# Layer-0 self attention of six tiles: softmax weights turned in 32x32 blocks by VectorE and moved between partitions by transfers, and a planner that chooses its pass by length and thinness

## The chip, the cores and the metric

The kernel runs on one core of a Trainium2 chip. The metric is the device time of one execution in microseconds. The kernel before was run ten times: median 2908.72 us, lowest 2903.48, highest 2914.35. Beside these there is one profiled execution of it.

## The reference

The program is a whole decoder of four layers on 32 sequences of 64 tokens with 256 features. Each layer adds self attention (or a state-space mixer in its place), cross attention to a context, and a feed-forward part to `x`, each on a layer-normalised `x`:

```python
x = x + _L0_attn_ref(_layernorm(x, axis=-1), L0_attn_wq, L0_attn_wk, L0_attn_wv, L0_attn_wo, ...)
x = x + _L0_xattn_ref(_layernorm(x, axis=-1), ctx_1024, mask_BxS2_bf1, ...)
x = x + _L0_ffn_ref(...)
...
```

The part that the change touches is the first line. With 32 query heads, 8 key and value heads and a head size of 64, what it returns is

```python
q, k = _apply_rope(q, cos, sin), _apply_rope(k, cos, sin)
scores = jnp.einsum('bhqd,bhkd->bhqk', q, k) / jnp.sqrt(jnp.float32(HD))
scores = jnp.where(causal[None, None], scores, jnp.finfo(scores.dtype).min)
probs = jax.nn.softmax(scores, axis=-1)
o = jnp.einsum('bhqk,bhkd->bhqd', probs, v)
return o.transpose(0, 2, 1, 3).reshape(b, s, NH * HD) @ wo.T
```

The weights `probs` come out with the queries on the partitions. The product with `v` sums over keys, and TensorE sums over partitions, so each block of weights has to be turned before that product.

## The kernel before

The 2048 tokens are 16 tiles of 128 rows, two sequences in each. `x` stays in the on-chip memory the whole time. A *unit* is one layer part on one or two tiles. `body` (from line 2606) records the units in an order of its own: the tiles go in groups of 8, 6 and 2 (`GROUPS`), and while a later group goes through the wide parts of layers 0 and 1, the group before it goes through the rest; `weave` mixes the two streams by shares. The first group has nothing beside it: its layer-0 self attention on tiles 0 to 7, then its layer-0 cross attention, stand alone at the start of the program.

Nothing is issued while units are recorded. The `Recorder` keeps each instruction with what it reads and writes, and the names of its buffers. Afterwards a planner, `Order`, simulates the five queues (TensorE, VectorE, ScalarE, GpSimd, and SP, which issues transfers) with a price for each instruction (`duration`), a start-up time for transfers, and a number of buffers per pool (`Net.SLOTS`): ten large ones of 4 KB a partition (`b4`), sixteen of 2 KB (`b2`), eight PSUM banks (`mm`), and others. It may look 120 us of TensorE's work ahead of the oldest unfinished instruction. An instruction with two possible engines (`either`: VectorE or ScalarE; `combine`: VectorE or GpSimd) is given to the one that ends first. Where TensorE would wait for more than 1.6 us and a bank is free, `fill` puts in a product that nobody reads (`spare`). A transfer is priced at 0.45 us on SP, and its result is held to be there 2 us or more later.

`in_turns` runs this planner forwards and backwards in alternation: each pass is renumbered by the one before it. With `rounds` 4 there are nine passes, of which five are forward. The forward pass with the shortest planned length is issued; all queues of the program then follow its order. On the chip, each queue works strictly in that order, waiting on semaphores.

All instructions are issued at one place (`issue`, line 2541), so the profile tells them apart by the names of tiles, which come from the function that made them.

A unit of layer-0 self attention (`unit_L0_attn`) works on tile `i`: a norm, projections with the rotation (`rope_mm`, `rope_b`), scores of 64x64 blocks into four PSUM banks, and then for each half `u` a softmax over a buffer of 128 partitions x 16 x 64. The partitions hold the queries. The scaled weights of a half are then turned by `turn`: eight 128x128 transposes on TensorE into two PSUM banks (`turn_mm`) and two evictions of 128x512 into one `b4` buffer (`turn_b`). The products with `v` read that buffer, 64 partitions at a time, two blocks of 128 columns for each:

```python
pT = self.turn(ss[u].rearrange("p a b -> p (a b)"), 8)
...
nc.tensor.matmul(po[64 * j : 64 * j + 64, hi, :], v[rb, kv * 64 : kv * 64 + 64],
                 pT[rb, j * 4 + hi * 2 : j * 4 + hi * 2 + 2, :], start=True, stop=True)
```

In cross attention the weights are turned differently, in 32x32 blocks by VectorE (`blocks`, tile name `blocks_b`), and the product takes the context's rows in strips of 32.

Of the kernel before, what the change touches and what calls it, by code (L numbers as in the profile page):

```python
# [26 lines left out]
P = 128  # L27
# [200 lines left out]
def split(ap, a, pat="p (a b) -> p a b"):  # L228
    return ap.rearrange(pat, a=a)
# [238 lines left out]
def part(method, args):  # L468

    if method == "transpose":  # L470
        return 128, 128
    return tuple(32 if n <= 32 else 64 if n <= 64 else 128 for n in (args[1].n, args[1].size()))
# [66 lines left out]
class Order:  # L539
# [81 lines left out]
    def run(self):  # L621
        ready = {e: [] for e in self.ENGINES}

        def enter(op):
            for e, _ in op.ways:
                bisect.insort(ready[e], op, key=lambda o: o.at)

        for o in self.ops:
            if o.waits == 0:
                enter(o)  # L630
        stuck, done, oldest, result, self.starts = False, [False] * len(self.ops), 0, [], {}
        while not all(done[oldest:]):
            limit = self.pos[oldest] + self.horizon
            best = None
            for e in self.ENGINES:
                now, seen, first = self.free_at[e], 0, 1e9
                for o in ready[e]:
# [9 lines left out]
                    start = max(now, since)  # L647
# [28 lines left out]
                    best = ((key, o.at), o, e, start, cost, opens)  # L676
# [7 lines left out]
            _, o, e, start, cost, opens = best  # L684
            filler = self.fill(o, start) if e == "tensor" else None
            if filler:
                o, start, opens = filler, self.free_at[e], []
# [9 lines left out]
            m = next(m for w, m in o.ways if w == e)  # L697
# [8 lines left out]
            if e == "scalar":  # L706
                m = next(m for w, m in o.ways if w == e)
# [14 lines left out]
            for n in o.after:  # L722
                same = len(n.ways) == 1 and n.ways[0][0] == e and o.ways[0][1] not in DMA
                at = (start if e in ("tensor", "sync") else got + 0.03) if same else got + lat
# [2 lines left out]
                n.waits -= 1  # L727
                if n.waits == 0:
                    enter(n)
            if not filler:  # L730
                done[o.at], self.starts[o] = True, (start, len(result))
            while oldest < len(done) and done[oldest]:
                oldest += 1
# [48 lines left out]
        o.after = before[o]  # L782


def in_turns(ops, slots, horizon, spare, rounds):

    best, ops = None, list(ops)
    for k in range(2 * rounds + 1):
        plan = Order(ops, slots, horizon, spare)
        result = plan.run()  # L790
        if k % 2 == 0 and (best is None or plan.length < best[0]):
            best = plan.length, result, {t: t.slot for o, _ in result for t in o.tiles}
        if k < 2 * rounds:
            backwards(ops)
            renumber(ops, plan.starts)
            rewind(ops)
    for t, slot in best[2].items():
        t.slot = slot
    return best[1]


class Net:
# [200 lines left out]
    def blocks(self, p, n):  # L1003
# [2 lines left out]
        self.nc.vector.transpose(pT.rearrange("p a h q -> p h a q"), p.rearrange("p h (a k) -> p h a k", a=2))  # L1006
        return pT

    def turn(self, p, n):

        pT = self.b4(n, P)
        for j in range(0, n, 4):
            ps = split(self.mm(), 4)
            for u in range(4):
                self.transpose(ps[:, u, :], p[:, (j + u) * P : (j + u + 1) * P])
            self.evac(pT[:, j : j + 4, :], ps)
        return pT
# [19 lines left out]
    def unit_L0_attn(self, layer, W, i):  # L1037
        nc = self.nc
        wq, wkv, wo = W
        cos, sin = (bc(v, 1, 8) for v in (self.k("rope0")[:, :64], self.k("rope0")[:, 64:]))  # L1040

        def rope(q, hT, cols):

            ps = self.mm()
            for x in range(4):
                self.prod(ps[:, x * P : (x + 1) * P], [(w, hT[:, c, :]) for c, w in enumerate(cols(x))])
            p3, t1, t2 = split(ps, 8), self.tmp(8, 64), self.tmp(8, 64)
            nc.vector.tensor_tensor(t1, p3, cos, ALU.mult)
            for j in range(4):
                at, of = (slice(32 * a, 32 * a + 32) for a in (j, j ^ 1))  # L1050
                self.evac(t2[at], p3[of])
            nc.combine(t2, t2, sin, ALU.mult)
            nc.combine(q, t1, t2, ALU.add)

        hT = self.norm(layer, [i])

        kk = self.b2(4, 2, 64)
        rope(kk.rearrange("p m b n -> p (m b) n"), hT, lambda x: [wkv[:, c, x * P : x * P + P] for c in range(2)])
        qs = [self.b4(2, 4, 2, 64) for _ in range(2)]
        for m in range(4):  # L1060
            rope(
                qs[m // 2][:, m % 2].rearrange("p g b n -> p (g b) n"), hT,
                lambda x: [wq[c][:, (4 * m + x) * P : (4 * m + x + 1) * P] for c in range(2)],
            )
        pv = self.mm()
        self.prod(pv, [(hT[:, c, :], wkv[:, c, 512:]) for c in range(2)])
        v = self.b2(512)
        self.evac(v, pv)

        sc = [self.mm() for _ in range(4)]  # L1070
        for u in range(2):
            for hi in range(2):
                for gp in range(2):
                    for b in range(2):
                        col = slice((hi * 2 + gp) * P + b * 64, (hi * 2 + gp) * P + b * 64 + 64)

                        for j in range(2):
                            r = slice(64 * j, 64 * j + 64)
                            for x in range(2):
                                nc.tensor.matmul(  # L1080
                                    sc[2 * u + j][64 * x : 64 * x + 64, col],
                                    qs[hi][r, u, 2 * gp + x, b],
                                    kk[r, 2 * hi + u, b],
                                    start=True,
                                    stop=True,
                                )
        ss = []
        for u in range(2):

            s = self.b4(16, 64)  # L1090
            for j in range(2):
                nc.vector.tensor_tensor(
                    s[:, 8 * j : 8 * j + 8], split(sc[2 * u + j], 8), bc(self.k("causal"), 1, 8), ALU.add
                )
            self.shift(s, s)
            nc.scalar.activation(s, s, AF.Exp, scale=0.125)
            r = self.weigh(s, s)
            nc.combine(s, s, bc(r, 2, 64), ALU.mult)
            ss.append(s)
        terms = []  # L1100
        for u in range(2):

            pT = self.turn(ss[u].rearrange("p a b -> p (a b)"), 8)

            oT = self.b4(2, 4, P)
            for b in range(2):
                po = split(self.mm(), 2)
                rb = slice(64 * b, 64 * b + 64)
                for hi in range(2):
                    for j in range(2):  # L1110
                        kv = hi * 4 + 2 * u + j
                        nc.tensor.matmul(
                            po[64 * j : 64 * j + 64, hi, :],
                            v[rb, kv * 64 : kv * 64 + 64],
                            pT[rb, j * 4 + hi * 2 : j * 4 + hi * 2 + 2, :],
                            start=True,
                            stop=True,
                        )
                self.evac(
                    oT[:, :, :, b * 64 : b * 64 + 64],  # L1120
                    po.rearrange("p h (g n) -> p h g n", n=64),
                )
            terms += [(oT[:, hi, c, :], wo[hi][:, u * 4 + c, :]) for hi in range(2) for c in range(4)]
        ps = self.mm()[:, :256]
        self.prod(ps, terms)
        self.outproj(i, ps)
# [1479 lines left out]
def body(tc, ins, out):  # L2606
    net = Net(ins, out)
    net.warm(8)
    for i in range(2):
        net.start(i)  # L2610

    at, before, ffn = 0, [], ["L1_queues"]
    for k, n in enumerate(GROUPS):
        tiles = range(at, at + n)
        wide = WIDE if k == len(GROUPS) - 1 else WIDE[:-1]
        if before:
            if wide is not WIDE:
                net.queues[at] = net.far(f"queue{k}", 8 * n * P, 256)
            early = NARROW[:4] if wide is WIDE else []
            weave(run_stages(net, ffn + NARROW, before), run_stages(net, wide + early, tiles))  # L2620
        else:
            weave(run_stages(net, wide[:2], tiles))
            net.queues[at] = net.far(f"queue{k}", 8 * n * P, 256)
            weave(run_stages(net, wide[2:4], tiles))
            net.slots = net.far("slots", 64 * P, ROW)
            weave(run_stages(net, wide[4:], tiles))
            net.parts = net.far("parts", 6 * QUEUED, 256)
        at, before = at + n, tiles

    net.all_experts, net.nc.quick = net.load_L3_experts(), True  # L2630
    weave(run_last(net, NARROW[4:-1], before), net.experts(QUEUED // P))
    issue(tc, in_turns(net.nc.ops, Net.SLOTS, 120.0, net.spare, 4), Net.SLOTS)


# [15 lines left out]
```

## Time and profile before

| what | value |
|---|---|
| median of ten runs | 2908.72 us (2903.48 to 2914.35) |
| profiled execution | 2915.26 us, span 2913.5 us |
| mean granted TensorE clock | 0.974 |
| busy: TensorE products | 2805.7 us |
| busy: VectorE | 2129.8 us |
| busy: ScalarE | 1518.5 us |
| busy: GpSimd | 1525.7 us |
| DMA | 259.04 MB, mean 89 GB/s |
| instructions | 66660 |

The page is one execution on the chip. A busy share is the time in which an engine had an instruction in work. Products are pipelined, so their listed durations overlap; what TensorE pays for one of a series is the spacing of their starts. The granted clock is the share of full speed at which TensorE was allowed to run, averaged over a slice. "Idle before" is the time that an engine stood still before an instruction, and the name behind the arrow is what released it. SPq is the queue that issues transfers. DMA times "to landing" go from the issue to the arrival of the data.

### The profile page before, as it was taken

To read this page: it belongs to the slowest core of one execution; us is meant where nothing else is said; L and a number is where in the kernel's file an instruction comes from. 1 tells how busy PE (TensorE), PEld (TensorE's weight loads), DVE (VectorE), ACT (ScalarE), POOL (GpSimd) and SP (SyncE) were. 2 spreads that over 40 slices of the span, in tenths; PEclk is the share of its full clock that TensorE was granted. 3 is DMA by queue.
4 is the path that set the end of the run, shared out by engine and by line. 5 is a ranking of instruction groups with operands and counts; after the bars stand their busy time and mean duration, and the time that the engine had idled before them with its cause. 6 is when DMAs were issued, how large, how long until landed. Compare 5 with 4: busy or idle time off the path is not lost.

```text
span 2913.5 us, 66660 instructions
## 1 busy us (share of the span) xinstructions
PE 2805.7 (96%) x26626; PEld 2338.6 (80%) x26626; DVE 2129.8 (73%) x5139; ACT 1518.5 (52%) x2849; POOL 1525.7 (52%) x1304
## 2 busy tenths in 40 slices
PE   8999999999999899999999999999999999999895
PEld 7888888878778788888878778878797878877674
DVE  5664457775777767867589998787846879988853
ACT  5554226665445454544366656665534665376550
POOL 6762232212666545424554437685715477457665
PEclk8999999999999999999999999999999999998977
DMA  4003320400261146122100110022374122211435
GB/s 179 16 13 116 139 109 19 156 1 31 81 259 46 57 152 203 62 64 69 46 17 30 33 56 17 8 96 77 127 263 171 57 73 82 89 51 58 143 113 176
DMA packets 120313, 259.04 MB, mean 89 GB/s; under 512 B 27077, under 2 KB 81880, under 8 KB 107588
## 3 DMA queue, kind: packets, MB, share of 16 engines
q1 hardware_dynamic: 110212, 230.68, 22.8%
q0 software_dynamic: 9792, 24.10, 2.4%
q8 instruction: 211, 3.46, 0.5%
q14 instruction: 98, 0.80, 0.1%
HBM read 179.38 MB, written 78.77 MB: 89 GB/s over the span
## 4 chain that ended last, share of the span: by engine, by line
PE 78%; DVE 11%; ACT 6%; POOL 2%; issue 2%; DMA 0%; SPq 0%; POOLq 0%; DVEq 0%; ACTq 0%
PE L_xattn_mm L2541 13%; PE ssm_heads_mm L2541 11%; PE pair_mm L2541 10%; PE cross_out_mm L2541 9%; PE L_attn_mm L2541 7%; PE L_ffn_mm L2541 5%; PE L_block_mm L2541 3%; PE rope_mm L2541 2%; PE turn_mm L2541 2%; DVE rope_b L2541 2%; PE L_dense_mm L2541 2%; PE cross_scores_mm L2541 2%; PE heads_mm L2541 2%; ACT rope_b L2541 2%; PE small_scores_mm L2541 1%
## 5 line engine op out<-in xcount | busy, mean ns | idle before, releaser
L2541 PE MATMUL pair_mm<-norm_b,load_ssm_w 128*128 128x256 f32 x1280 | 307.1, 381 | 1.5 <-DVE __init___x L2541 0.5
L2541 PEld LDWEIGHTS pair_mm<-norm_b,load_ssm_w 128*128 128x128 f32 x1280 | 235.0, 190 | 36.8 <-issue 4.5
L2541 POOL TENSOR_TENSOR L_xattn_sm<-L_xattn_sm,__init___consts 128x8 f32<-128x8 f32 (+2 forms) x64 | 190.5, 2983 | 57.2 <-DVE L_xattn_sm L2541 50.4
L2541 DVE SCALAR_TENSOR_TENSOR ssm_heads_b<-pair_mm,load_ssm_wp,ssm_heads_b 128x252 f32<-128x252 f32 (+2 forms) x480 | 196.9, 465 | 22.5 <-ACT ssm_heads_b L2541 21.4
L2541 ACT COPY rope_b<-rope_mm 32x512 f32<-32x512 f32 x234 | 134.7, 577 | 115.7 <-DVE rope_b L2541 71.9
L2541 POOL TENSOR_TENSOR norm_sm<-norm_sm,__init___consts 128x1 f32<-128x1 f32 (+1 forms) x149 | 93.9, 640 | 169.3 <-DVE norm_sm L2541 149.8
L2541 ACT ACT_TABLE_LOAD x136 | 174.5, 1283 | 10.7 <-DVE L_xattn_sm L2541 2.6
L2541 ACT COPY L_xattn_b<-L_xattn_mm 128x512 f32<-128x512 f32 x177 | 103.8, 591 | 130.9 <-PE L_xattn_mm L2541 128.0
L2541 PE MATMUL rope_mm<-norm_b,load_L_attn_w 128*128 128x128 f32 x1280 | 163.1, 282 | 4.3 <-DVE rope_b L2541 2.7
L2541 PEld LDWEIGHTS rope_mm<-norm_b,load_L_attn_w 128*128 128x128 f32 x1280 | 155.6, 197 | 13.8 <-issue 8.1
L2541 PE MATMUL ssm_heads_mm<-load_ssm_w,ssm_heads_b 128*128 128x256 f32 x640 | 160.0, 384 | 0.2 <-DVE ssm_heads_b L2541 0.2
L2541 ACT ACTIVATE ssm_heads_b<-ssm_heads_b 128x512 f32<-128x512 f32 (+1 forms) x152 | 124.3, 833 | 51.3 <-DVE ssm_heads_b L2541 37.0
L2541 POOL TENSOR_TENSOR ssm_heads_b<-ssm_heads_b,ssm_heads_b 128x1024 f32<-128x1024 f32 x33 | 80.7, 2451 | 134.4 <-DVE ssm_heads_b L2541 115.8
L2541 PEld LDWEIGHTS ssm_heads_mm<-load_ssm_w,ssm_heads_b 128*128 128x128 f32 x640 | 116.5, 190 | 23.1 <-issue 9.3
L2541 POOL TENSOR_TENSOR rope_b<-rope_b,__init___consts 128x512 f32<-128x512 f32 x72 | 93.2, 1296 | 79.2 <-DVE rope_b L2541 37.3
L2541 ACT COPY turn_b<-turn_mm 128x512 f32<-128x512 f32 x194 | 106.4, 602 | 53.2 <-PE turn_mm L2541 50.4
L2541 DVE TENSOR_SCALAR norm_b<-__init___x,norm_sm,norm_sm 128x256 f32<-128x256 f32 x192 | 104.8, 565 | 31.5 <-POOL norm_sm L2541 9.6
L2541 PEld LDWEIGHTS L_xattn_mm<-norm_b,load_L_xattn_w 128*128 128x128 f32 x1024 | 121.1, 192 | 7.8 <-issue 5.9
L2541 ACT COPY norm_b<-norm_mm 128x256 f32<-128x256 f32 (+1 forms) x133 | 56.9, 436 | 133.1 <-PE norm_mm L2541 118.7
L2541 POOL TENSOR_TENSOR heads_b<-heads_b,heads_sm 128x1024 f32<-128x1024 f32 x52 | 102.0, 1969 | 45.6 <-DVE heads_sm L2541 26.0
L2541 PE MATMUL L_xattn_mm<-norm_b,load_L_xattn_w 128*128 128x128 f32 x1024 | 125.4, 276 | 0.0
L2541 PEld LDWEIGHTS L_xattn_mm<-norm_b,units_L_xattn_w 128*128 128x128 f32 x1024 | 119.9, 192 | 3.3 <-issue 1.0
(439 smaller groups left out, 7895.4 us busy)
## 6 DMA issues: line engine op xcount, KB each, us to landing
L_block_w<-in_f_rows SPq DMA_DIRECT2D x42, 770.0 KB, 5.9
queue<-far_w SPq DMA_DIRECT2D x14, 1024.0 KB, 10.7
load_ssm_w<-in_s_in SPq DMA_DIRECT2D x12, 1024.0 KB, 6.4
parts<-far_w SPq DMA_DIRECT2D x10, 1024.0 KB, 17.1
slots<-far_w SPq DMA_DIRECT2D x16, 548.0 KB, 7.7
L_experts_b<-slots SPq DMA_DIRECT2D x32, 274.0 KB, 5.1
units_L_xattn_w<-kept_x SPq DMA_DIRECT2D x8, 1024.0 KB, 7.9
L_parts_b<-parts SPq DMA_DIRECT2D x14, 512.0 KB, 8.5
```

The source lines that it names most:

```text
L2541: done = getattr(getattr(nc, e), method)(*map(real, op.args), **kw)
```

## The change

It has three parts.

First, for tiles 2 to 7 (six tiles of the first group) `turn` is replaced by `moved`. VectorE turns the whole buffer of a half, 128 partitions x 1024, in blocks of 32x32 within strips of 32 partitions, into a `b4` buffer `y`. Sixteen transfers, issued by SP, then carry block row `a` of column block `b` to partitions 32b to 32b+31 of a second `b4` buffer `z`; each is 32 partitions x 1 KB. The other ten tiles keep `turn`.

Second, the product's view of the turned weights is rewritten so that it fits both: runs of 32 queries, four of them to a block of 128. The numbers in PSUM lie as before.

Third, the planner's choice. `in_turns` gets 8 rounds instead of 4: 17 passes, nine of them forward. Instead of the shortest, the pass with the least `plan.length + THIN * thin(plan)` is issued. `thin` cuts the plan into stretches of 3.413 us, adds up TensorE's planned work in each, fillers included, and counts the stretches with less than 36% of work. `THIN` is 3 us a stretch.

```diff
         stuck, done, oldest, result, self.starts = False, [False] * len(self.ops), 0, [], {}
+        self.fills = []
...
-            if not filler:
+            if filler:
+                self.fills.append(start)
+            else:
                 done[o.at], self.starts[o] = True, (start, len(result))
...
+STRETCH, FULL, THIN = 3.413, 0.36, 3.0
+
+def thin(plan):
+    work = {}
+    for o, (start, _) in plan.starts.items():
+        if o.ways[0][0] == "tensor":
+            k, m = part(o.ways[0][1], o.args)
+            n = o.args[2].size() * 0.00167 * k * m / P**2 if o.ways[0][1] == "matmul" else 0.107
+            at = int(start / STRETCH)
+            work[at] = work.get(at, 0.0) + n
+    for start in plan.fills:
+        work[int(start / STRETCH)] = work.get(int(start / STRETCH), 0.0) + 0.43
+    return sum(work.get(i, 0.0) < FULL * STRETCH for i in range(max(work)))
...
-        if k % 2 == 0 and (best is None or plan.length < best[0]):
-            best = plan.length, result, {t: t.slot for o, _ in result for t in o.tiles}
+        worth = plan.length + THIN * thin(plan)
+        if k % 2 == 0 and (best is None or worth < best[0]):
+            best = worth, result, {t: t.slot for o, _ in result for t in o.tiles}
...
+    def moved(self, p, n):
+        y, z = self.b4(4, n, 32), self.b4(4, n, 32)
+        self.nc.vector.transpose(y.rearrange("p b j q -> p j b q"), p.rearrange("p (j b k) -> p j b k", j=n, b=4))
+        for b in range(4):
+            for a in range(4):
+                self.nc.sync.dma_start(out=z[32 * b : 32 * b + 32, a], in_=y[32 * a : 32 * a + 32, b])
+        return z.rearrange("p a j q -> p j a q")
...
-            pT = self.turn(ss[u].rearrange("p a b -> p (a b)"), 8)
+            p = ss[u].rearrange("p a b -> p (a b)")
+            pT = self.moved(p, 8) if i in range(2, 8) else self.turn(p, 8).rearrange("p j (a q) -> p j a q", q=32)
...
-                            po[64 * j : 64 * j + 64, hi, :],
+                            po[64 * j : 64 * j + 64, hi, :].rearrange("p (g a q) -> p g a q", g=2, q=32),
...
-    issue(tc, in_turns(net.nc.ops, Net.SLOTS, 120.0, net.spare, 4), Net.SLOTS)
+    issue(tc, in_turns(net.nc.ops, Net.SLOTS, 120.0, net.spare, 8), Net.SLOTS)
```

## The prediction

> **What bounds the kernel now.** I read the page's busy shares first, then the granted clock in slices, then a table of stages, and inside the first stage the tiles of the turned weights and the order in time. The page:
>
> ```profile
> PE 2805.7 (96%) x26626; PEld 2338.6 (80%) x26626; DVE 2129.8 (73%) x5139; ACT 1518.5 (52%) x2849; POOL 1525.7 (52%) x1304
> ...
> PEclk8999999999999999999999999999999999998977
> ...
> PE 78%; DVE 11%; ACT 6%; POOL 2%; issue 2%; DMA 0%; SPq 0%; POOLq 0%; DVEq 0%; ACTq 0%
> ```
>
> TensorE is busy for 2805.7 of 2913.5 us and carries 78% of the chain of waits. All its idle time is 107.8 us; nothing but less TensorE work, less of that idle time, or less time at a reduced clock can move the end much. The stages (stretch, length, then busy us and count for PE, PEld, DVE, ACT, POOL, then granted clock, DMA share, GB/s):
>
> ```profile
> 0.00:250.00 250.00, 235.99 (x2512) 208.40 (x2513) 148.37 (x250) 134.70 (x238) 162.00 (x124) 0.95 0.22 78
> 250.00:900.00 650.00, 649.04 (x5487) 534.97 (x5486) 417.62 (x938) 299.47 (x522) 228.59 (x163) 1.00 0.26 97
> 900.00:1250.00 350.00, 328.73 (x3176) 284.01 (x3178) 275.44 (x650) 180.87 (x337) 189.82 (x158) 0.98 0.34 111
> 1250.00:1950.00 700.00, 689.64 (x6861) 572.50 (x6854) 565.94 (x1360) 408.65 (x778) 379.77 (x336) 1.00 0.12 41
> 1950.00:2150.00 200.00, 192.17 (x1754) 160.62 (x1753) 151.23 (x412) 100.97 (x198) 119.03 (x97) 0.95 0.37 127
> 2550.00:2913.50 363.50, 312.52 (x3238) 246.73 (x3236) 251.00 (x739) 179.63 (x364) 231.80 (x228) 0.88 0.33 108
> ```
>
> Layer-0 self attention of the first eight tiles lies in the first row. TensorE idles 14.0 us there, 21.3 from 900 to 1250, and 51.0 in the last row, which also has the worst clock. A finer cut shows how the clock is lost:
>
> ```profile
> 60.00:70.00 10.00, 9.37 (x126) 8.99 (x127) 9.70 (x18) 5.33 (x9) 7.96 (x7) 0.66 0.01 2
> 170.00:180.00 10.00, 8.76 (x78) 7.17 (x79) 7.00 (x9) 4.53 (x7) 7.69 (x6) 0.66 0.09 28
> 1500.00:1510.00 10.00, 7.71 (x83) 6.87 (x84) 7.37 (x17) 4.36 (x7) 5.73 (x4) 0.66 0.01 2
> 2650.00:2660.00 10.00, 8.09 (x84) 6.09 (x83) 8.70 (x18) 7.61 (x21) 10.00 (x8) 0.50 0.01 2
> ```
>
> A clock of 0.66 over 10 us is 3.4 us of full-speed time lost. Adding (1 - clock) x 10 us over all 10 us slices gives 12 us before 250, 20 us in seven separate places from 900 to 2550, and 31 us from 2640 to 2880. That, 51 us behind the first stage, is what a choice by thin stretches can reach for.
>
> **The turned weights, removed.** Six tiles lose 16 turns each, 96 in all:
>
> ```profile
> L2541 PE MATMUL turn_mm<-__init___consts,L_attn_b x256: 272/273/447, 72.1 to 2115.1; 128*128 128x128 f32 x128
> L2541 ACT COPY turn_b<-turn_mm x194: 562/591/767, 75.7 to 2800.1; 128x512 f32<-128x512 f32 x194
> ...
> 82.68 0.87 PE turn_mm L2541 x8
> ...
> 114.69 1.04 PE L_attn_mm L2541 x16
> ```
>
> 256 turns are 16 tiles' worth. The 273 ns are a pipelined matmul's length; the chain shows what TensorE pays, 0.87 us for eight, 0.109 each. So 96 x 0.109 = 10.5 us of TensorE's work go. With them go 24 evictions x 0.591 = 14.2 us, mostly ScalarE's, which is busy 112 of the 200 us from 50 to 250, and that is worth nothing by itself.
>
> **What VectorE gets.** Two block turns per tile, priced by the same shape in cross attention:
>
> ```profile
> L2541 DVE STREAM_TRANSPOSE blocks_b<-L_xattn_b x32: 1196/1235/1247, 269.4 to 2461.3; 128x1024 f32<-128x1024 f32 x32
> ```
>
> 12 x 1.235 = 14.8 us. From 50 to 250 VectorE is busy 121 of 200 us, so it has room: cost 0. If its order were tight, as from 60 to 70 where it is busy 9.7 of 10, a turn there would cost its 1.2 us; twelve times that, 15 us, is the upper end.
>
> **What the transfers cost.** Each half of a tile issues 16 transfers of 32 partitions x 1 KB, 192 in all, 6.3 MB. The trace has no transfer between partitions of the on-chip memory. Nearest rows: issues one behind another on SP, and small transfers' landing:
>
> ```profile
> 329.34 0.43 SPq L2541 DMA_DIRECT2D load_ssm_ws<-in_s_in  x1
> 329.81 0.47 SPq L2541 DMA_DIRECT2D load_ssm_wp<-in_s_dtb  x1
> ...
> context_cx<-in_ctx SPq DMA_DIRECT2D x64, 64.0 KB, 2.0
> ```
>
> One issue per 0.47 us makes 16 x 0.47 = 7.5 us per half, 15 us per tile, 90 us of SP. The turned weights are whole 1.24 + 7.5 + 2.0 = 10.7 us after the scaled weights, against 0.87 + two evictions of 0.59, about 2 us, before: 8.7 us later. The 2.0 us can be 1.7 (output rows) or, behind bulk loads, 17.1 (zeros into the queue of parts); DMA is at 0.00 to 0.01 between 50 and 120, so I take 2.0. Does the delay show? In the order in time, taking the turns in pairs as tiles, tile 4's turns are at 154 and 156 and their products at 166 to 174, tile 7's at 236 and 240 and theirs after 250: there some 10 us lay between anyway. Tile 2's turns at 96 and 105 had products at 101 and 115, and tile 3's at 128 and 131 had them at 132 and 136, so there it must be covered by the next tile's projections, about 7 us (60 at 0.11), and its scores. A tile passes every 21 us (72 to 240 for eight). I take 0, because the planner sees the transfer's length and may run ahead; the upper end is 8.7 us for each of six tiles, 52 us.
>
> A rule speaks against this. The Trainium skill, "VectorE: DVE Perf Modes", section "Rules for kernel authors", tells authors to turn 128x128 on TensorE where a PSUM destination will do, and keeps VectorE for 32x32 blocks. Followed, it would count the 10.5 us as no gain and the later weights as a loss, up to 52 us. Another, "DMA: Bandwidth & Descriptors", section "Rules for kernel authors", says that a transfer under 64 KB is mostly overhead, with some 2.0 us fixed by its section on the anatomy of a DMA; taken in series, 192 would be an estimated 384 us. The rows put 0.47 us between issues, so the fixed parts overlap.
>
> SP is in order: behind a transfer that waits for VectorE's turn stand the operand loads of layer-0 cross attention (128 to 191 us) and its contexts from 210. SP idles most of 50 to 128 and 138 to 191, so I charge 0. POOL's queue issues nothing more.
>
> **Buffers.** The pool of ten large buffers gives two to a half instead of one, the added one from VectorE's turn to the last transfer's end, some 10 us. A tile holds two for queries, two for scores, two for outputs; next tile's two queries still fit. I charge 0; if they do not, the stall is in the 52 us above.
>
> **The products of the turned weights** read runs of 32 instead of 128. No row shows that shape; 16 such products take 1.04 us now, and the element count is unchanged, so 0; were they to take double, 6 x 32 x 0.065 = 12.5 us more. Nothing suggests a gain.
>
> **What of the 10.5 us reaches the end.** In 60 to 80 and 160 to 180, 40 of the 190 us, TensorE was not the limit; there it buys nothing. 10.5 x 150/190 = 8.3, I take 8 us. From 250 to 900 TensorE idles 1 us, so time won before is passed on, not lost in a later wait.
>
> **The pass.** Nine forward passes instead of five are compared, by length plus 3 us per thin stretch, and the chosen one orders the whole program anew. The most to be had is 51 us of clock and the idle time with it. A thin stretch removed is worth 3.4 us of clock at most, and up to 3 us of planned length may be paid for it. I take four fewer at about 2 us net, 8 us. Ends: 0 (the shortest is also the least thin) or a loss of 12 (four paid for with 3 us, none seen on the chip), and 35 us if most of the 51 go.
>
> **Sum.** The profiled execution took 2915.3 us, 1.8 more than its span. 2915.3 - 8 - 8 = 2899.3. It was 6.5 us above the median 2908.7, so a median of 2892.8: 2893.
>
> **Rivals.**
> - *A luckier order.* The half-clock stretches in 2640 to 2880 and at 950, 1505 and 2003 go, 25 us instead of 8, beside the 8 of TensorE: 2876. For it: the last stage has 31 us of lost clock in some eight places. Against it: that stage ends narrow, with 51 us of idle that no reordering removes while work is missing.
> - *Hidden both ways.* The 10.5 us turn into idle time, since the weights are late by as much, and the pass gives nothing: 2908.7 within 5.8 us, which is the 0.2% that a measurement of this kernel can tell from no change. For it: two stretches of the stage are already bound by the elementwise chain. Against it: the other 150 us.
> - *Late weights stall TensorE (slower).* From 50 to 240, with TensorE waiting for transfers or for a large buffer. Decides from 1.74 us of stall per moved tile (what 16 turns save), plus 3.4 us whenever the gap also drops the clock. At 3 us of stall and one clock drop in each of six tiles: 6 x 6.4 - 8 = 30, less 8 for the pass, +22: 2931. For it: tile 2's products came 5 to 10 us after their turn, tile 3's 4 and 5. Against it: the gaps of tiles 4 and 7.
> - *The choice does nothing.* The pass of least worth is also the shortest: 2915.3 - 8 - 6.5 = 2901, still slightly faster.
>
> **How the numbers follow.** Forecast 0.32 (2886 to 2898); choice does nothing 0.10, all but its upper edge faster; luckier order 0.18; hidden 0.14; slower 0.26. Faster is 0.32 + 0.10 + 0.18 = 0.60, same 0.14, slower 0.26, for which an order that is worse elsewhere counts too. To leave out two in ten I go from 2866 (luckier order with 35 instead of 25) to 2932 (the stall's price). The likeliest case's own range is 2886 to 2898.
>
> **What would show it.** Right: 96 fewer turns and 192 more issues on SP in the changed trace, 12 block turns at 1.2 us, TensorE's busy time 10 us less, fewer 10 us slices under 1.0. Wrong: idle TensorE before the products of the turned weights released by a transfer; clock below 0.95 in the first 250 us; issues well above 0.5 us; products above 0.066 us each; more idle time after 900 than the 93 us of now.

## The result, and the profile after

The changed kernel takes 2943.72 us (median of 13 runs, 2931.8 to 2956.11) against 2910.64 us for the kernel before (45 runs): ratio 1.0114, 95% interval 1.0100 to 1.0129. It is 33 us slower. The forecast was 2893 us, faster.

The page after, its own lines of the span, of busy time, of TensorE's clock in 40 slices, and of one group of products:

```profile
span 2945.8 us, 66818 instructions
...
PE 2826.7 (96%) x26536; PEld 2354.6 (80%) x26536; DVE 2131.7 (72%) x5122; ACT 1526.4 (52%) x2867; POOL 1513.4 (51%) x1294
...
PEclk9999999999999899999999999999899999998997
...
L2572 PE MATMUL pair_mm<-norm_b,load_ssm_w 128*128 128x256 f32 x1280 | 315.4, 390 | 0.0
```

The last group in the page before:

```profile
L2541 PE MATMUL pair_mm<-norm_b,load_ssm_w 128*128 128x256 f32 x1280 | 307.1, 381 | 1.5 <-DVE __init___x L2541 0.5
```

TensorE has 90 instructions fewer (96 turns gone, 6 filler records more) and is busy 21 us longer. Its work did not grow: products that the change does not touch, such as `pair_mm`, take longer in the mean (390 ns, 381 before), because more of them run at half clock. The mean clock fell from 0.974 to 0.964. As time lost that is (1 - 0.974) x 2913.5 = 76 us before and (1 - 0.964) x 2945.8 = 106 us after, 30 us more. TensorE's idle time went from 107.8 to 2945.8 - 2826.7 = 119.1 us, 11 us more. With 10.5 us of work less, 30 + 11 - 10.5 = 31 us, against 32.3 us between the two spans. So the whole loss is clock and idle time.

Where is it? Fixed stretches of time hold different work in the two kernels, so I cut both where TensorE has the same work still to come (its products without fillers, each at the spacing of its shape in the kernel before). The rows have length, busy time of PE, PEld, DVE, ACT and POOL, granted clock, DMA. The kernel before:

```profile
0.00:386.90 386.90, 372.89 (x3842) 328.44 (x3846) 215.29 (x380) 174.14 (x319) 198.54 (x148) 0.97 0.27 97
386.90:1012.90 626.00, 615.94 (x5222) 504.21 (x5215) 443.87 (x1045) 320.51 (x559) 262.44 (x194) 0.99 0.22 83
1012.90:1665.90 653.00, 634.78 (x5861) 539.45 (x5861) 503.18 (x1197) 342.88 (x643) 316.62 (x288) 0.99 0.23 75
1665.90:2334.60 668.70, 655.31 (x6253) 543.26 (x6248) 527.09 (x1347) 385.09 (x725) 377.62 (x331) 0.98 0.27 95
2334.60:2913.50 578.90, 526.77 (x5461) 423.24 (x5459) 440.33 (x1173) 295.92 (x606) 370.47 (x345) 0.92 0.30 98
```

The changed kernel:

```profile
0.00:387.40 387.40, 368.93 (x3755) 321.59 (x3756) 227.47 (x375) 176.46 (x320) 194.66 (x144) 0.96 0.33 116
387.40:1040.20 652.80, 638.52 (x5272) 520.99 (x5271) 439.89 (x1050) 323.01 (x557) 265.34 (x198) 0.97 0.21 78
1040.20:1681.90 641.70, 631.64 (x5816) 538.22 (x5815) 491.38 (x1201) 354.25 (x659) 319.93 (x294) 0.99 0.24 77
1681.90:2357.10 675.20, 660.73 (x6217) 545.70 (x6216) 529.47 (x1326) 376.64 (x720) 363.22 (x319) 0.97 0.28 94
2357.10:2945.80 588.70, 526.88 (x5484) 428.14 (x5482) 443.52 (x1174) 296.06 (x615) 370.29 (x342) 0.93 0.29 97
```

Two things are to be seen. The first row holds all of the moved weights. It has 10.5 us less work and takes 0.5 us longer: idle time grew from 14.0 to 18.5 us, and the clock is lower. The second row holds cross attention, feed-forward and state-space work of layers 0 and 1, which the change does not touch. It takes 26.8 us longer: TensorE is busy 22.6 us longer with the same work (and twelve filler records), at a clock of 0.97 instead of 0.99, and idle 4.2 us longer. Its half-clock stretches add up to 41 us there, in the kernel before to 7; half of each is lost, so some 17 of the 26.8 us are lost clock. The other three rows add -11.3, +6.5 and +9.8.

The transfers themselves, in the changed kernel; first durations (least, median, greatest) of the issues and the block turns, then the queue SP in order of time, then the landing:

```profile
L2572 SPq DMA_DIRECT2D moved_b<-moved_b x192: 507/589/1642, 102.6 to 248.3; - x192
L2572 DVE STREAM_TRANSPOSE moved_b<-L_attn_b x12: 1202/1234/1246, 101.4 to 221.4; 128x1024 f32<-128x1024 f32 x12
...
DMA to landing us min/median/max: 1.9/1.9/3.5
```

```profile
102.63 21.59 SPq L2572 DMA_DIRECT2D moved_b<-moved_b  x32
...
161.39 23.53 SPq L2572 DMA_DIRECT2D moved_b<-moved_b  x32
...
203.77 45.07 SPq L2572 DMA_DIRECT2D moved_b<-moved_b  x64
```

An issue takes 0.59 us, and 32 in a row take 21.6 us, 0.675 each. SP spends 132 of the 146 us from 103 to 249 on them. I had put 0.47, and the planner 0.45. Two halves of a tile make 2 x 10.8 = 21.6 us of SP, and a tile passes every 21 us: SP has no slack, and a half has to wait for the one before it. The twelfth block turn ends at 222.7 us, and the last transfer of its half is issued at 248.3.

### The profile page after: what moved, and what is told of

The parts are those of the page before. It is cut to its first block, busy times and chain, and to the rows that moved or that the text cites. A ratio compares the mean times of both kernels' runs of the same rounds, so it can differ in the third digit from the quotient of the medians.

```text
span 2945.8 us, 66818 instructions
## 1 busy us (share of the span) xinstructions
PE 2826.7 (96%) x26536; PEld 2354.6 (80%) x26536; DVE 2131.7 (72%) x5122; ACT 1526.4 (52%) x2867; POOL 1513.4 (51%) x1294
## 4 chain that ended last, share of the span: by engine, by line
PE 49%; DVE 5%; ACT 3%; issue 2%; POOL 1%; DMA 0%; POOLq 0%; DVEq 0%; ACTq 0%
PE L_xattn_mm L2572 7%; PE ssm_heads_mm L2572 7%; PE pair_mm L2572 6%; PE cross_out_mm L2572 4%; PE L_attn_mm L2572 3%; PE L_ffn_mm L2572 3%; PE turn_mm L2572 3%; PE L_block_mm L2572 2%; PE heads_mm L2572 2%; PE L_dense_mm L2572 2%; PE outrows_mm L2572 1%; PE L_expert_mm L2572 1%; PE L_experts_mm L2572 1%; PE small_scores_mm L2572 1%; PE small_values_mm L2572 1%
## 5 line engine op out<-in xcount | busy, mean ns | idle before, releaser
L2572 PE MATMUL pair_mm<-norm_b,load_ssm_w 128*128 128x256 f32 x1280 | 315.4, 390 | 0.0
L2572 ACT COPY rope_b<-rope_mm 32x512 f32<-32x512 f32 x266 | 153.3, 577 | 119.8 <-DVE rope_b L2572 65.7
L2572 DVE SCALAR_TENSOR_TENSOR ssm_heads_b<-pair_mm,load_ssm_wp,ssm_heads_b 128x252 f32<-128x252 f32 (+2 forms) x480 | 195.9, 465 | 10.8 <-ACT ssm_heads_b L2572 10.0
L2572 ACT COPY L_xattn_b<-L_xattn_mm 128x512 f32<-128x512 f32 x163 | 95.7, 589 | 153.4 <-PE L_xattn_mm L2572 143.4
L2572 PE MATMUL L_attn_mm<-load_L_attn_w,L_attn_b 128*128 128x256 f32 x512 | 124.4, 391 | 0.6 <-ACT L_attn_b L2572 0.6
L2572 PE MATMUL cross_out_mm<-load_L_xattn_w,cross_out_b 128*128 128x256 f32 x512 | 121.8, 386 | 0.0
```

The source lines that it names most:

```text
L2572: done = getattr(getattr(nc, e), method)(*map(real, op.args), **kw)
```

## The experiments

Three theories. A: a pass that the planner has worked over more often loses more on the chip. B: the moved weights come late and stall TensorE. C: every new order of the program is a draw of its own, and the order of the kernel before was a good one. The times of the kernel before were 2908 to 2911 us in two of the series and 3004 to 3010 us in the three others, on other chips; each ratio is to the kernel before in its own series.

### Passes, with and without moving

Four edits of the changed kernel. This is e1; e4 has 6 in place of 4:

```diff
-    issue(tc, in_turns(net.nc.ops, Net.SLOTS, 120.0, net.spare, 8), Net.SLOTS)
+    issue(tc, in_turns(net.nc.ops, Net.SLOTS, 120.0, net.spare, 4), Net.SLOTS)
```

e2 has the first pair of lines, e3 both:

```diff
-            pT = self.moved(p, 8) if i in range(2, 8) else self.turn(p, 8).rearrange("p j (a q) -> p j a q", q=32)
+            pT = self.moved(p, 8) if i in () else self.turn(p, 8).rearrange("p j (a q) -> p j a q", q=32)
...
-STRETCH, FULL, THIN = 3.413, 0.36, 3.0
+STRETCH, FULL, THIN = 3.413, 0.36, 0.0
```

> The changed kernel with 4 rounds instead of 8: the moved weights stay, the pass is the best of five. If the later passes cost the time (theory A: a pass that the planner has worked over more often is tighter in the plan and loses more clock on the chip), it takes 2895 to 2912, lost clock 70 to 85 us as before. If the moved weights cost it (theory B: they come late and stall TensorE in the first 250 us), it takes 2935 to 2950. If each order is a draw of its own (theory C), anything from 2895 to 2950, with the difference in lost clock and idle time spread over the program.

> The changed kernel with all sixteen tiles turned by TensorE as before; 8 rounds, choice by length and thin stretches. Theory A: 2930 to 2950, since a later pass is chosen. Theory B: 2900 to 2915, since nothing is moved. Theory C: anything from 2895 to 2950.

> As the one with all tiles turned and 8 rounds, but THIN 0: choice by length alone, which takes the last pass. Theory A: 2935 to 2955, more than with thin stretches counted. Theory B: 2900 to 2915. Theory C: anything from 2895 to 2950, with no relation to the plan's length.

> The changed kernel with 6 rounds instead of 8: the moved weights stay, another pass is issued. Theory A: between the one of 4 rounds and the changed kernel, 2910 to 2935. Theory B: 2935 to 2950, as the changed kernel. Theory C: anything from 2895 to 2950.

Measured: e1 1.0102 (1.0067 to 1.0138), e2 1.0068 (1.0039 to 1.0098), e3 1.0007 (0.9984 to 1.0029), e4 1.0061 (1.0043 to 1.0079).

A falls: e3 issues the last pass of all, the most worked over, and is even with the kernel before, while e1, an early pass (the ninth of all), loses 1.0%, as much as the changed kernel lost in the result and more than the 0.4% that it loses in e5 below. B alone falls with e2, which moves nothing and is 0.7% slower. The choice by thin stretches did nothing in the changed kernel: the planner's own numbers for its forward passes show that the last one is both the shortest and the one of least worth, so length alone would have issued the same program. (These are plan figures, not times of a chip.)

```
changed kernel, forward pass 8, 12, 14, 16: planned length 2682.0, 2673.7, 2675.4, 2662.1; thin stretches 10, 9, 9, 9
kernel before, pass 8 (the one issued): 2683.6; thin stretches 9
```

The plan promised 21.5 us less than that of the kernel before; the chip took 33 us more.

### The order alone, and the transfers alone

e7 and e8 are the kernel before with one number changed (`in_turns(net.nc.ops, Net.SLOTS, 118.0, ...)` and `122.0`). e5 is the changed kernel again. e6 is the changed kernel, every other instruction in its place, with this in `issue`. It leaves out the move between partitions: of the sixteen transfers of a half one is issued, from all 128 partitions of `y` to the same partitions of `z`:

```diff
+            if e == "sync" and op.outs and op.outs[0].t.name.startswith("moved"):
+                z, y = op.outs[0].t, op.ins[0].t
+                if z not in whole:
+                    whole.add(z)
+                    a, b = (View(t, 0, P, 0, [(1, 1024)], F32).ap() for t in (z, y))
+                    nc.sync.dma_start(out=a, in_=b)
+                continue
```

> The changed kernel itself, beside the next three on one chip, as the measure for them. Ratio to the kernel before 1.008 to 1.014 by every theory. The issues of the 192 transfers last 0.59 us each again.

> The changed kernel in its own order, every instruction in its place, but of the sixteen transfers of a half only the first is issued, as one of 128 partitions x 4 KB; the weights are then not moved between partitions, which is left out. SP is free after 0.6 us instead of 11 us per half, the turned weights are whole some 10 us earlier. If the slow issue on SP is what keeps the 10.5 us from the end (theory B, narrowed to the first stage), it is 8 to 15 us faster than the changed kernel, all of it won before 400 us, and still slower than the kernel before by 15 to 25 us, ratio 1.005 to 1.009. If the transfers cost nothing (theory C alone, the order), within 3 us of the changed kernel. If they cost all of the 33 us, ratio below 1.002.

> The kernel before with nothing of the change, only the planner's horizon 118 us instead of 120: another order of the same instructions. Theory C (any new order loses what the order of before happened to have): ratio 1.002 to 1.010. Theories that blame the moved weights or the later passes: 0.998 to 1.002.

> The kernel before with nothing of the change, only the planner's horizon 122 us instead of 120. Theory C: ratio 1.002 to 1.010. The others: 0.998 to 1.002.

Measured: e5 1.0040 (1.0025 to 1.0055), e6 1.0000 (0.9979 to 1.0021), e7 1.0071 (1.0047 to 1.0096), e8 1.0132 (1.0089 to 1.0175).

e7 and e8 hold none of the change and lose 0.7 and 1.3%, e8 more than the 1.0% that I had put as the end. That is theory C, shown: an order of the same work costs this much by itself. e6 against e5 is the transfers' price with the order held: 14 us in the medians, and in the traces 17.3 us, all in the first stretch. The two rows are e5 and e6 up to the same remaining work:

```profile
0.00:387.30 387.30, 366.51 (x3755) 319.66 (x3756) 227.92 (x375) 176.40 (x320) 194.61 (x144) 0.97 0.34 116
```

```profile
0.00:370.00 370.00, 358.57 (x3755) 315.78 (x3756) 228.30 (x375) 175.82 (x320) 195.56 (x144) 0.99 0.33 121
```

With one transfer a half the stretch is 17 us shorter: 20.8 us of idle time become 11.4, and the clock rises.

How do the transfers cost 17 us? e5 and e6 issue their products in the same order, so each can be set beside its twin. e5 falls behind in two places: by some 9 us between 121 and 165 us, and by 6 more between 254 and 264. The changed kernel on the first chip has the same waits from 40 to 300 us (waited for: us, times, longest; then an entry of SP's queue):

```profile
PE L_attn_mm L2572 <- DVE L_attn_b L2572: 4.7, 2, 2.8
PE cross_out_mm L2572 <- DVE L_attn_b L2572: 2.4, 1, 2.4
...
DVE L_xattn_b L2572 <- DMA L_xattn_cx<-in_mask: 10.3, 2, 8.2
...
248.89 1.24 SPq L2572 DMA_DIRECT2D L_xattn_cx<-in_mask  x2
```

The 2.8 us are TensorE's wait at 146.7, before products of moved weights. The view names VectorE, but in e6, where that VectorE instruction has the same place in the order, the same products start ahead of it and without a wait. What they need is the first eight transfers of their half, and the eighth was issued at 144.6 and lands some 1.9 us later: the wait is for the transfers. In the second place TensorE waits for no moved weights at all. A load of the cross-attention mask stands on SP behind the last 64 transfers; VectorE waits 8.2 us for it and 2.1 for the next one (in e6 no such wait is longer than 0.7), and TensorE 2.4 us for VectorE. With each of TensorE's two waits comes a half-clock stretch that e6 does not have.

So B is right about the first stretch, though some 6 of the 17 us came through SP's queue and VectorE and not through the products of the moved weights. Behind the first stretch the transfers cost nothing more. By its ratio alone e6 fits the case "they cost all of the loss", and it does not show the 15 to 25 us that I had expected for the order: on this chip the changed kernel loses 13 us in all. The order's loss shows when the trace is cut: up to the work that the kernel before has done at 1012.9 us, the second row takes 648.9 us in e5 and 650.6 in e6, against 626.0 before.

e5's ratio is below what I expected; the same program loses 0.4% on one chip and 1.1% on the other. The two traces of it, cut at the same remaining work, run within 8 us of each other up to 2000 us, and at the end e5 is 71 us behind. Why, these runs do not settle.

### Keeping TensorE busy, and the right price

In these traces half-clock stretches follow 3.4 us of thin work (counted in the last section), so e9 (changed kernel) and e10 (kernel before) put unread products into the finished order wherever the planned work of the 3.4 us before falls under 40% of the array. The core of it:

```diff
+            missing = LIMIT * WINDOW - sum(w for _, w in recent)
+            while missing > 0 and now > 4:
...
+                out.append((f, "tensor"))
+                recent.append((now, 0.43))
+                missing -= 0.43
```

e11 prices the transfers as measured, in `duration`:

```diff
+        if isinstance(out, View) and isinstance(kw.get("in_"), View):
+            return 0.67
```

> The changed kernel in its own order, with 68 products that nobody reads put in where the planned work of the 3.4 us before falls under 40% of the array. They are 29 us of TensorE's work at full clock. If the half-clock stretches that follow thin work are what makes one order slower than another (theory C with the clock as its mechanism), lost clock falls by 30 us or more and the time by 5 to 25 us against the changed kernel. If the thin work is not the cause, lost clock stays and the time grows by 10 to 29 us.

> The kernel before in its own order, with 59 such products (25 us of work) by the same rule. Clock as the mechanism: ratio 0.993 to 1.000, less to win than in the changed kernel since its order has fewer half-clock stretches. Otherwise 1.003 to 1.009.

> The changed kernel, but the planner prices a transfer between partitions at 0.67 us on SP, as measured, not 0.45. It is another order. If the wrong price cost the first stage its gain, the work that the kernel before has done at 387 us is done 5 to 12 us earlier than in the changed kernel. If SP simply has too much to issue (130 us in 146), no earlier than 3 us. The whole time is a new draw: ratio 1.000 to 1.013.

> The kernel before itself, for its profile on this chip: 3000 to 3010 us if the chip is that of the earlier runs, and the first 2000 us within 5 us of its profile on the first chip, with the difference in the last stages.

Measured: e9 1.0237 (1.0192 to 1.0281), e10 1.0051 (1.0028 to 1.0075), e11 1.0080 (1.0052 to 1.0108). e12 ran on a chip as fast as the first, not on a slower one, so it says nothing of those: 2918.66 us, span 2916.9, clock 0.974, as the first profile.

e9 is a miss. Its clock is 0.966, 101 us lost where 106 were, and its median of 2975.84 us is 32 us above the changed kernel's in the result, a little more than the 29 us of the added products. e10's clock rose from 0.974 to 0.980, some 17 us won for 25 us of work; it lost 0.5%. A likely reason, not tested, is that the chip drifts from the plan, so that products placed by the plan fall beside the thin places. That thin work drops the clock is to be seen below; that it could be cured this way is refuted.

e11 hits the first stretch and misses the rest:

```profile
0.00:371.50 371.50, 361.08 (x3712) 317.39 (x3714) 213.94 (x355) 179.60 (x333) 191.67 (x143) 0.99 0.35 118
371.50:1013.40 641.90, 629.10 (x5266) 517.23 (x5261) 448.79 (x1058) 316.01 (x544) 279.26 (x205) 0.98 0.22 80
```

The stretch takes 371.5 us, 15.9 less than in the changed kernel and 15.4 less than before, though SP has as much to issue; I had expected 5 to 12. Its second row, untouched work in a new order, takes 641.9 us against 626.0, and the lead is gone by 1013 us.

### The order kept behind the first stage

Open was whether the loss behind the first stage is nothing but order. e13 plans only the first 260 planned us anew, with the moved weights and the price 0.67, and behind that issues the kernel before instruction by instruction, with its buffers. The new plan of the first part is a single forward pass that looks 60 us ahead (`AHEAD`). e15 is e13 at the price 0.45; e14 moves nothing.

```diff
+    old, new = record(ins, out, ()), record(ins, out, range(2, 8))
+    issue(tc, spliced(old, new), Net.SLOTS)
...
+    order, starts = in_turns(a_ops, slots, 120.0, old.spare, 4, 0.0)
+    soon = lambda o: o in starts and o.ways[0][0] == "tensor" and starts[o][0] < CUT
+    last = max(k for k, (o, _) in enumerate(order) if soon(o))
...
+    plan = Order(first, slots, AHEAD, new.spare)
+    result = plan.run()
...
+    for o, e in order[last + 1 :]:
+        if o in twin:
+            result.append((twin[o], e))
```

> Weights of tiles 2 to 7 moved, an issue priced at 0.67 us, only the first 260 planned us planned anew, and behind that the order of the kernel before, instruction by instruction. Theory C (the loss behind the first stage is the order): 3 to 15 us faster than the kernel before, ratio 0.995 to 0.999. If the moving itself costs time later: ratio 1.005 or more.

> As e13, with an issue priced at 0.45 us as in the changed kernel. If the wrong price ate the gain of the first stage, 5 to 15 us slower than e13, ratio 0.999 to 1.003. If the price does not matter, as e13.

> The control: the first 260 planned us planned anew, nothing moved, the order of the kernel before behind that. Ratio 0.998 to 1.002 by every theory.

Measured: e13 0.9965 (0.9951 to 0.9979), e15 1.0075 (1.0056 to 1.0094), e14 1.0030 (1.0019 to 1.0041).

e13 is faster than both kernels. Its rows, cut as above, and then those of e15:

```profile
0.00:377.70 377.70, 365.02 (x3746) 316.75 (x3750) 220.07 (x383) 169.83 (x306) 196.10 (x146) 0.99 0.34 116
377.70:1006.30 628.60, 617.51 (x5222) 506.17 (x5215) 442.95 (x1045) 320.35 (x559) 262.69 (x194) 0.99 0.22 82
```

```profile
0.00:408.90 408.90, 377.05 (x3750) 325.26 (x3754) 224.97 (x381) 171.44 (x309) 194.57 (x145) 0.95 0.32 107
408.90:1040.40 631.50, 620.72 (x5223) 508.03 (x5216) 442.42 (x1045) 320.52 (x559) 263.01 (x194) 0.99 0.22 82
```

In both, the second row takes 628.6 and 631.5 us, as the 626.0 of the kernel before and not as the 652.8 of the changed one. So in the stage where the changed kernel lost most, the loss was the order. The other runs agree. Cut the same way, this row takes 636 to 650 us in the four new orders that move nothing (e2, e3, e7, e8), 633 to 653 in the changed kernel, its repeat e5 and the three other new orders that move (e1, e4, e11), and 629 to 633 in the three that keep the old order (e13 to e15). e13 gains 10 us on the kernel before, inside the 3 to 15 that I expected; e15 is 29 us slower than e13, where I expected 5 to 15. The first rows differ by 31 us, and TensorE's waits from 40 to 300 us in e15 say why (waited for: us, times, longest):

```profile
PE L_attn_mm L2661 <- DMA moved_b<-moved_b: 14.1, 5, 4.6
PE L_attn_mm L2661 <- ACT L_attn_b L2661: 4.4, 2, 3.2
```

e13 has no wait for moved weights in that list. With the price at 0.45 the products stand in TensorE's queue too early; idle time over the whole first row is 31.9 us (408.9 - 377.05) against e13's 12.7, and the clock is 0.95 against 0.99. The control e14 missed its range: one forward pass over the first stage, nothing moved, is 8.6 us slower there (395.5 us) than the order that five forward passes had found. Against it, moving is worth 377.7 - 395.5 = -17.8 us. But the first stage is a draw too: cut the same way, the six orders that move nothing (the kernel before, e2, e3, e7, e8, e14) take 379 to 396 us there, the two that move at the price of 0.67 take 371.5 (e11) and 377.7 (e13), and the four that move at 0.45 take 387 to 409 (the changed kernel, e1, e4, e15). At 0.67 both lie below all six, e13 by only 1 us; how much of its gain is the moving and how much its draw is not shown.

## Why the prediction was wrong, point by point

**What TensorE loses and VectorE gets** held: 96 turns fewer, twelve block turns at 1.234 us against 1.235 foreseen, VectorE with room. The products in runs of 32 cost nothing more: sixteen listed at 1.11 us, as before. The rule that the prediction held against itself, to turn 128x128 on TensorE, is not borne out in e13: with the issue priced as measured and the order held behind the first stage, six tiles turned by VectorE are 0.35% faster.

**"What the transfers cost", taken at 0, is the first step that failed.** The row it rested on (one issue per 0.47 us, transfers from HBM) was not the price of these transfers: 0.675, so the weights were whole 1.2 + 10.8 + 1.9 = 13.9 us after the scaled ones at the least, not 10.7, and later where SP was still at the half before. (The 2.0 us that the prediction quotes from the Trainium skill, "DMA: Bandwidth & Descriptors", are stated in its section "Anatomy of one DMA" for transfers that GpSimd issues. These, issued by SP, landed in 1.9.) The reason given for 0 was that the planner sees the transfer's length; it saw 7.2 us of issue where the chip took 10.8. In the prediction's own sum 15 us of SP per tile leave slack in 21; the measured 21.6 us leave none. With that the next charge of 0 failed as well, "SP is in order": the mask behind the transfers held VectorE for 8.2 us and TensorE for 2.4. The prediction's list of gaps also left out tile 5, whose products before came 4 and 7 us after their turns. Measured, the transfers cost 17 us in the changed order (e5 against e6), inside the 52 us that I had named as the end. At the price of 0.67 the view shows no wait of TensorE for moved weights in e13, and the first stretch is 15 us shorter in e11.

**"What of the 10.5 us reaches the end", 8 us, failed with it**: nothing did, the first stretch is even.

**"The pass", taken at -8, failed in sign, and it is most of the miss.** Thinness chose nothing. Behind the first stage the changed kernel loses 32 us: 26.8 in the second row, where the order is shown to be the cause, and 5 in the three rows behind it, which no run holds apart. That is 40 of the 51 us between 2893 and 2943.72. I had bounded the loss at 12 by counting stretches that the choice trades; the bound should have come from what any other order costs. Four full reorderings of the same work, with nothing moved (e2, e3, e7, e8), lie between 0.07 and 1.3% above the kernel before, none below; e3's 0.07% is no difference that can be told from none. The stretch of the kernel before from 250 to 900, which the prediction showed, has a clock of 1.00 and 1 us of idle time in 650: a new order could not gain there, only lose.

**The rivals.** "The choice does nothing" was true and did not lead to its 2901. "Late weights stall TensorE" named a true cost and its place, but only part of its way (SP's queue took the rest) and not the size of the result: in the changed kernel it only cancels the 10.5 us. A worse order was mentioned in half a sentence, without a price; it should have been the rival on the other side.

What stays open: why the loss is 1.1% on one chip and 0.4% on the other, and what makes one order keep its clock. The traces say where the chips differ: on the slower ones the work behind 1666 us takes some 77 us more in e5 than in the changed kernel on the first chip, and some 80 us more in e13 than in the kernel before, whose order it has there. So the slower chips take nearly the same from both orders, and late. What the order costs behind the first stage is not the same either: 32 us on the first chip, and 14 between e5 and e13. The count of thin stretches in the plan (9 in both) did not tell them apart.

## What to carry to other kernels

Where an order is the pick of a search and the chip has timed it, an edit that lets the search run again puts the whole program to a new draw; price that draw as a term of its own, from a few reorderings that change nothing else, and test the edit with the order held wherever it does not reach. A planner's price for a new kind of instruction must be measured before the order is trusted: at 0.45 instead of 0.67 us on a queue, the first stage of e15 is 31 us longer than that of e13. A plan that is 21 us shorter by its own numbers is no evidence where the clock that it leaves out costs 76 us.

## What of the hardware was not expected

An issue on SP of a transfer between partitions of the on-chip memory (32 partitions x 1 KB) takes 0.59 us, 0.675 from one to the next, against 0.43 and 0.47 for the two loads from HBM that the prediction went by. In e6 the issue of one transfer of 128 partitions x 4 KB, sixteen times the bytes, takes only 0.47 us. The landing, 1.9 us, is near the 2.0 of the 64 KB loads.

The clock can halve with TensorE busy throughout. Two stretches of 3.4 us of the changed kernel, and TensorE's order in time across them:

```profile
1702.10:1705.50 3.40, 3.40 (x119) 3.40 (x120) 3.18 (x9) 1.27 (x3) 0.00 (x0) 1.00 0.02 5
1705.50:1708.90 3.40, 3.40 (x33) 3.01 (x31) 3.21 (x14) 0.37 (x1) 0.00 (x0) 0.50 0.00 0
```

```profile
1702.06 4.21 PE L2572 MATMUL heads_mm<-values_b,turn_b 128*64 128x18 f32 x128
```

In the first stretch TensorE runs products of 18 columns on half of the array, one behind another, and is busy for all of it; the next 3.4 us are granted half clock. Busy time does not show what this clock answers to: in the 3.4 us before the drop TensorE is never idle at eight of the changed kernel's 28 half-clock stretches, and at three of the 19 of the kernel before. Weighted work shows it better. All half-clock stretches in these two traces but the last, which the end of the program cuts, last a multiple of 3.41 us, so I cut the traces into windows of that length in step with them, and count each product by its columns and by the share of the array that it uses (256 columns on the whole array take 0.21 us). In the changed kernel 17 of the 18 windows at full clock with less than 30% of work are followed by half clock, and none of the 737 with 45% or more; in the kernel before, 14 of 16 and none of 757.
